# A four-layer graph megakernel: x loaded in chunks in turn, accumulating writes of one expert declared independent, and part of the edge counting placed under the first mixture

## The chip, the core and the metric

One Trainium2 chip, one core of it. The metric is the device time of one execution in microseconds (us). The kernel before takes 2444.24 us, the median of 8 runs (2439.33 to 2447.27).

TensorE (PE in the profile) multiplies matrices, VectorE (DVE) and ScalarE (ACT) work elementwise and empty the matmul accumulators (PSUM), GpSimd (POOL) does some elementwise work and issues the indirect transfers, and SyncE (SP) issues most plain transfers. Each engine runs its own queue of instructions in order, and semaphores tie the queues together.

## The reference

2708 nodes with 256 features each (`x`, f32) and a sparse 0/1 adjacency matrix pass through four layers. Each layer adds a graph block and then a feed-forward block, each on the layer norm of x:

```python
x = x + _L0_gnn_ref(_layernorm(x), adj, Wq, Wk)          # cosine attention over neighbours
x = x + _L0_ffn_ref(_layernorm(x)[None], ...)[0]         # pooled tokens through a state-space block
x = x + _L1_gnn_ref(_layernorm(x), adj, weight, bias)    # mean over neighbours, then a projection
x = x + _L1_ffn_ref(_layernorm(x)[None], ...)[0]         # first mixture: 8 experts, top 2
x = x + _L2_gnn_ref(_layernorm(x), adj, W, a)            # graph attention, 1 head
x = x + _L2_ffn_ref(_layernorm(x)[None], ..., edge_index)[0]  # second mixture, 4 experts
x = x + _L3_gnn_ref(_layernorm(x), adj, W, a)            # graph attention, 4 heads
x = x + _L3_ffn_ref(_layernorm(x)[None], ...)[0]         # third mixture: 8 experts with a capacity
```

Three pieces matter here. The first mixture is, for every expert `e` with hidden size 1024,

```python
h = gelu(xf @ W1[e] + b1[e])
out = out + w_dense[:, e:e+1] * (h @ W2[e] + b2[e])      # w_dense: softmax over the two best gates
```

The layer-2 attention projects the layer norm with a 256 x 256 matrix, scores each edge as leaky_relu(source + target), takes a softmax over the neighbours and aggregates.

The second mixture chooses its experts with a small attention over `edge_index`, a list of 1,048,576 (source, target) pairs drawn from 65,536 nodes. Only edges whose target is one of the 2708 nodes given here count; where the source is none of them either, it stands for a node whose features are zero. So for each target a count of such edges is needed (`cnt`), and the few edges with both ends inside are needed one by one.

## The kernel before

**x and the layer norm.** x stays in SBUF for the whole kernel as 22 tiles of 128 nodes (`self.x`, 128 x 22 x 256 f32; the last tile has 20 rows). Most passes go over `CHUNKS`, six chunks of up to 512 nodes (four tiles; the last has one full tile and the tail of 20). At the start (L52 to L64) the first four tiles come one by one, in turn from the queues of SyncE and ScalarE, and the rest as three transfers of four tiles, one of five and the tail, all of SyncE. The layer norm of a chunk is a statistic per tile on VectorE (`ln_st`, L1617, `ln_mv`, L1618), a square root on ScalarE and a reciprocal and a shift on VectorE (L1620 to L1622), and the scaled rows `fa` (L1629 on ScalarE, L1631 on VectorE). TensorE transposes `fa` (`ft_ps`, L1587; `f_ps` in layer 0), the copies `fT` empty it, and the projection follows (`wqk` in layer 0, L1706; `v_ps`, L3389, in layer 2).

**The first mixture, `fast_l1_ffn` (L3198).** Each of the eight experts has 768 slots: six tiles (`TPE`) of 128 tokens, handled as two halves of three tiles (`HT`). `Route` (from L2835) ranks the tokens, and writes for every slot the row to gather (`idg`) and the row to add to (`ids`). For a half, three indirect transfers on GpSimd gather the tokens (`xe`, L2954), TensorE transposes them (`xt_ps`, L3228; `turn`), `k.copy` empties the accumulator into `xT`, turn about on VectorE (L76) and ScalarE (L78), the up product runs (`h_ps`, L3242, 16 matmuls) with its gelu on ScalarE (`hT`, L3249), and the down product (`y_ps`, L3259, 24 matmuls). VectorE adds the bias and multiplies by the gate (`ys`, L3267 and L3268), and an indirect transfer on GpSimd adds each tile of `ys` to the rows of `acc` in DRAM (L3271), 48 such accumulating writes in all. `acc` holds x itself beforehand, so afterwards it is the new x. Empty slots point to spare rows behind the nodes' rows, one per partition (`p1n`, L2930, `number`, L2978). All these writes go to one tensor, so each waits for the landing of the one before. After the last, seven transfers of three tiles and the tail bring `acc` back into `self.x` (L3326 to L3333).

**The side work.** `Edges` finds and counts the edges of the second mixture. `search` (L2561) is a generator of eight steps: each loads a piece of `edge_index`, builds a key per edge inside the range, and takes the best 72 keys of each partition with nine rounds of maximum and replacement on VectorE (L2585, L2586), into `L`, 128 x 576. `count` (L2592) is a generator too. It splits the keys into the target's high and low part and the source (L2610 and on), takes the up to 32 keys per partition with both ends inside in four rounds, ranks them over partitions (`rank_oh`, L2686, `rank_oc`, L2693, `rank_ov` on GpSimd, L2701, 32 matmuls L2708), and then, for 18 groups of 32 key columns, builds two one-hot arrays on VectorE:

```python
                oh = hot.tile([128, HB, 128], BF16, name="oh")
                ol = hot.tile([128, HB, NT], BF16, name="ol")
                for out, val, n in ((oh, lob, 128), (ol, hib, NT)):
                    nc.vector.tensor_tensor(
                        out,
                        io[:, None, :n].to_broadcast([128, HB, n]),
                        val[:, s0 : s0 + HB, None].to_broadcast([128, HB, n]),
                        ALU.is_equal,
                    )
```

(L2745 to L2752), whose product, 32 matmuls of 22 columns (L2756), is added into `cnt_ps`. The one-hots have two buffers, so a pair waits for the matmuls of the pair two before. A copy gives `cnt`.

`fast_l1_ffn` is given `search` as its side work and takes one step after each expert (`next(side)`, L3323); the loop after it empties what is left. `count` is given to the layer-2 attention, `fast_gat` (L3336), which takes a step between its pieces.

**The layer-2 attention.** The preamble: weights and the small products `pr` and `w` (L3373, L3379), layer norm and projection of all chunks (`V`, `fs`), the maximum over nodes, exponentials, the scaling of `V` on GpSimd (L3416), and the spreading of the row values over partitions (`spread_ps`, L118; the copies `Rr`, L76 and L78). The body: for every chunk of targets and each of 21 source tiles an adjacency tile `aj` is loaded, VectorE makes `PT` (L3459), and TensorE adds `acc_ps` (L3528).

**What orders the work.** The engine queues are written by a tile framework whose recording layer lays out the instructions of several generators side by side by planned times; within one engine the order is fixed when the kernel is built. Dependences between instructions are found from the tiles that they touch.

Of the kernel before, what the change touches and what calls it, by code (L numbers as in the profile page):

```python
# [1 line left out]

# [5 lines left out]
F32 = mybir.dt.float32  # L8
# [4 lines left out]
ALU = mybir.AluOpType  # L13
# [30 lines left out]
class K:  # L44
# [3 lines left out]
    def __init__(self, ctx, tc, x_in):  # L48
# [6 lines left out]
        for t in range(4):  # L55
            (nc.scalar if t % 2 else nc.sync).dma_start(
                self.x[:, t, :], x_in[t * 128 : (t + 1) * 128]
            )
        for t0, n in ((4, 4), (8, 4), (12, 4), (16, 5)):
            nc.sync.dma_start(  # L60
                self.x[:, t0 : t0 + n, :],
                x_in[t0 * 128 : (t0 + n) * 128].rearrange("(t p) d -> p t d", p=128),
            )
        nc.sync.dma_start(self.x[:TAIL, NT - 1, :], x_in[(NT - 1) * 128 : N])  # L64
# [5 lines left out]
        nc.vector.memset(self.eps, 1e-5)  # L70

# [2464 lines left out]
class Edges:  # L2536
# [55 lines left out]
    def count(self):  # L2592
        nc, tc = self.k.nc, self.k.tc
        with tc.tile_pool(name="ep", bufs=1) as pp, tc.tile_pool(
            name="eh", bufs=2
        ) as hot, tc.tile_pool(name="ps_eh", bufs=1, space=PSUM) as ps:
# [53 lines left out]
            rp = ps.tile([128, 5 * OW], F32, name="rank_ps")  # L2650
# [93 lines left out]
            cp = ps.tile([128, NT], F32, name="cnt_ps")  # L2744
# [90 lines left out]
class Route:  # L2835
# [14 lines left out]
    def __init__(self, k, ctx, w, most):  # L2850
# [10 lines left out]
        self.acc = dram.tile([N + 1 + 128, D], F32, name="acc")  # L2861
# [22 lines left out]
        nc.gpsimd.dma_start(self.acc[N + 1 :, :], zero[:, :D])  # L2884
# [45 lines left out]
        self.p1n = pool.tile([128, 1], F32, name="p1n")  # L2930
        nc.vector.tensor_scalar(self.p1n, self.p1, float(N), None, ALU.add)
# [32 lines left out]
    def early(self):  # L2964

        v = self.k.nc.vector
        bad = self.k.bad[:, 6:7]
        v.tensor_scalar(bad, self.sofar[:, 0:1], -1.0, float(HT * 128), ALU.mult, ALU.add)
        f = self.one.tile([128, 2, HT], F32, name="early_f")
        idf, idp = f[:, 0, :], f[:, 1, :]  # L2970
        v.scalar_tensor_tensor(
            idf, self.slot_f[:, 1, :HT], 128.0, self.slot_f[:, 2, :HT], ALU.mult, ALU.add
        )
        self.number(idf, idp, self.idg0, self.ids0)
        self.xe0 = self.gather(self.idg0, self.most * 128 + 1)
        yield

    def number(self, idf, idp, idg, ids):  # L2978

        v = self.k.nc.vector  # L2980
        v.tensor_copy(idg, idf)
        v.tensor_scalar(idp, idf, 0.0, self.p1n, ALU.is_equal, ALU.mult)
# [215 lines left out]
def fast_l1_ffn(k, side, route, rest):  # L3198
# [8 lines left out]
    with ExitStack() as ctx:  # L3207
# [3 lines left out]
        ps1 = ctx.enter_context(tc.tile_pool(name="ps_f11", bufs=3, space=PSUM))  # L3211
        ps2 = ctx.enter_context(tc.tile_pool(name="ps_f12", bufs=2, space=PSUM))

        def psum():
            return pst.tile([128, 512], F32, name="xt_ps")

        class Half:
# [5 lines left out]
            def turn(self):  # L3223
                self.xT = dp.tile([128, 2, HC], F32, name="xT")
                for kk in range(2):
# [7 lines left out]
                    k.copy(self.xT[:, kk, :], tp[:, :HC])  # L3233
# [20 lines left out]
            def down(self):  # L3254
                _, _, w2t, b2t = route.weights[self.e]
                for i in range(HT):
# [14 lines left out]
                    nc.gpsimd.indirect_dma_start(  # L3271
# [7 lines left out]
                    )  # L3279
                    yield  # L3280
# [25 lines left out]
        side = side(route.start)  # L3306
        nxt = [one, half(0, 1)]
        run(first)
        for e in range(E):
# [13 lines left out]
            next(side)  # L3323
        for _ in side:
            pass
        for t0 in range(0, NT - 1, 3):  # L3326
            nc.sync.dma_start(
                k.x[:, t0 : t0 + 3, :],
                acc[1 + t0 * 128 : 1 + (t0 + 3) * 128].rearrange(
                    "(t p) d -> p t d", p=128  # L3330
                ),
            )
        nc.sync.dma_start(k.x[:TAIL, NT - 1, :], acc[1 + (NT - 1) * 128 : 1 + N])  # L3333
# [1090 lines left out]
def model(tc, I, out):  # L4424
# [4 lines left out]
    with tc.tile_pool(name="flags", bufs=1) as fp:  # L4429
# [4 lines left out]
        with ExitStack() as ctx:  # L4434
# [5 lines left out]
            with tc.tile_pool(name="lists", bufs=1) as lp:  # L4440
                edges = Edges(k, part(I, "L2_ffn_"), lp)
                order = (0, 1, 5, 2, 3, 4)
                with ExitStack() as c1:
# [18 lines left out]
                    fast_l1_ffn(k, edges.search, route, rest)  # L4462
                fast_gat(
                    k, adjT, I["L2_gnn_W"], I["L2_gnn_a"], 1, True, 2, edges.count()
# [76 lines left out]
```

## Time and profile before

| | us |
|---|---|
| median of 8 runs | 2444.24 (2439.33 to 2447.27) |
| the profiled run | 2442.74 |
| its span, first to last instruction | 2440.9 |
| mean granted TensorE clock | 0.952 |

The profiled run is one of the usual ones, 1.5 us under the median; 1.84 us of it lie outside the span. Of the span, this is what TensorE and VectorE are busy in each stage:

| stage | us from the start | length | TensorE busy | VectorE busy | clock |
|---|---|---|---|---|---|
| start and layer-0 projection | 0 to 60 | 60.0 | 43.99 | 40.98 | 1.00 |
| layer-0 attention | 60 to 340 | 280.0 | 280.00 | 117.10 | 1.00 |
| layer-0 feed-forward | 340 to 562 | 222.0 | 202.23 | 140.65 | 0.89 |
| layer-1 graph block, with most of the routing | 562 to 790 | 228.0 | 214.81 | 113.77 | 0.97 |
| end of the routing, start of expert 0 | 790 to 820 | 30.0 | 26.85 | 14.12 | 0.94 |
| rest of the first mixture, reload of x | 820 to 1184.7 | 364.7 | 334.84 | 259.50 | 0.97 |
| layer-2 attention, preamble | 1184.7 to 1238.3 | 53.6 | 36.72 | 50.90 | 0.75 |
| layer-2 attention, body | 1238.3 to 1465 | 226.7 | 221.47 | 210.66 | 0.99 |
| second mixture | 1465 to 1740 | 275.0 | 269.92 | 89.36 | 0.93 |
| layer-3 attention, start of the third mixture | 1740 to 2230 | 490.0 | 440.44 | 394.49 | 0.94 |
| rest of the third mixture | 2230 to 2440.9 | 210.9 | 194.27 | 105.66 | 0.97 |

A row of a timeline gives the start and the length in us, the engine, the source line, the operation, what it writes and reads, and how many instructions the row holds; in square brackets is the idle time of the engine before it and what ended that. A row of a window gives its bounds and length, the busy time of TensorE, of its weight load, of VectorE, ScalarE and GpSimd (instructions in brackets), the granted TensorE clock, the busy share of the DMA engines and GB/s. A group's row gives the smallest, median and largest duration in ns and the first and last start.

### The profile page before, as it was taken

The page shows a single profiled execution, that of the slowest core. Times are in us where ns is not written, and L with a number is a line of the kernel's source. Part 1 is how long each engine was busy: PE and PEld are TensorE (multiplying, and loading weights), DVE is VectorE, ACT ScalarE, POOL GpSimd, SP SyncE. Part 2 cuts the span into 40 slices and gives each one's busy share as a digit, 9 for nine tenths or more (in the row PEclk, how much of TensorE's full clock was granted, in tenths as well). Part 3 has the DMA queues.
Part 4 walks back from the last instruction along what each step waited for, and adds up shares of the span by engine and source line. Part 5 has one row for each costly group of instructions (what it writes and reads, how often), then busy time and mean ns, then how long its engine had stood idle before and what let it go on. Part 6 is the DMA issues. An engine that isn't in the chain of part 4 may idle for free. (4 is left out here: it accounts for less than half of the span.)

```text
span 2440.9 us, 31809 instructions
## 1 busy us (share of the span) xinstructions
PE 2265.6 (93%) x11620; PEld 1513.2 (62%) x11620; DVE 1537.2 (63%) x3419; ACT 659.3 (27%) x1329; POOL 419.5 (17%) x490
## 2 busy tenths in 40 slices
PE   7999999988999899999689999999889999968997
PEld 4677775677778566767578876666553333325665
DVE  6444338655446699961598994152579999863544
ACT  5433333214664222122310003232321111111121
POOL 2000003004000324332150001620030000002321
PEclk9999999879999899999889996999999999978998
DMA  4233322200664444341254423000024433315340
GB/s 129 65 99 96 100 61 77 74 1 11 217 210 131 144 111 118 86 95 24 65 166 128 145 54 58 21 1 1 10 67 116 117 113 112 95 43 170 118 133 14
DMA packets 158380, 219.34 MB, mean 90 GB/s; under 512 B 30879, under 2 KB 94083, under 8 KB 158212
## 3 DMA queue, kind: packets, MB, share of 16 engines
q1 hardware_dynamic: 125856, 179.58, 25.0%
q0 software_dynamic: 15248, 23.39, 4.6%
q10 hardware_dynamic: 17108, 14.22, 1.8%
q8 instruction: 96, 1.57, 0.3%
q14 instruction: 72, 0.59, 0.1%
HBM read 193.49 MB, written 24.17 MB: 89 GB/s over the span
## 5 line engine op out<-in xcount | busy, mean ns | idle before, releaser
L3459 DVE SCALAR_TENSOR_TENSOR PT<-Rr,Q,aj 128x512 f32<-128x512 f32 (+3 forms) x630 | 405.5, 702 | 25.5 <-PE acc_ps L3528 13.7
L3605 PE MATMUL acc_ps<-PT,V 128*64 128x512 f32 (+4 forms) x2016 | 328.5, 549 | 0.4 <-ACT Rr L78 0.4
L3605 PEld LDWEIGHTS acc_ps<-PT,V 128*64 128x64 f32 (+1 forms) x2016 | 95.2, 122 | 210.1 <-issue 154.6
L1819 PE MATMUL acc_ps<-fa,PT 128*128 128x257 f32 x882 | 213.9, 382 | 0.5 <-DVE PT L1793 0.5
L1819 PEld LDWEIGHTS acc_ps<-fa,PT 128*128 128x128 f32 x882 | 164.6, 190 | 63.8 <-issue 41.0
L3528 PE MATMUL acc_ps<-V,PT 128*128 128x257 f32 x882 | 198.6, 385 | 1.5 <-POOL V L3416 0.9
L3528 PEld LDWEIGHTS acc_ps<-V,PT 128*128 128x128 f32 x882 | 167.3, 192 | 28.5 <-DVE PT L3459 2.4
L3242 PE MATMUL h_ps<-xT,w1t 128*128 128x384 f32 x512 | 173.3, 497 | 5.1 <-DVE xT L76 4.9
L1793 DVE SCALAR_TENSOR_TENSOR PT<-aj,PT 128x512 f32<-128x512 int32 (+1 forms) x126 | 80.1, 643 | 147.8 <-ACT PT L1792 147.7
L3259 PE MATMUL y_ps<-w2t,hT 128*128 128x256 f32 x768 | 168.6, 379 | 0.0
L2478 PE MATMUL acc_ps<-V,at 128*128 128x257 bf16 x1323 | 157.9, 278 | 3.6 <-DVE at L2472 3.6
L3259 PEld LDWEIGHTS y_ps<-w2t,hT 128*128 128x128 f32 x768 | 145.4, 190 | 21.4
L2478 PEld LDWEIGHTS <-at 128*128 128x128 bf16 x1323 | 130.0, 100 | 26.5 <-issue 5.0
L3242 PEld LDWEIGHTS h_ps<-xT,w1t 128*128 128x128 f32 x512 | 97.8, 194 | 72.5 <-DVE xT L76 6.3
L1792 ACT ACTIVATE PT<-s_ps,rq 128x512 f32<-128x512 f32 (+1 forms) x126 | 79.4, 637 | 168.0 <-PE s_ps L1768 166.9
L3271 POOL DMA_INDIRECT acc<-ys,ids x48 | 77.8, 1620 | 237.8 <-DVE ys L3268 117.5
L1768 PE MATMUL s_ps<-KT,QT 128*128 128x512 f32 (+1 forms) x252 | 116.4, 546 | 0.9 <-POOL KT L1747 0.6
L3951 PE MATMUL y_ps<-w2t,hT 128*128 128x256 f32 (+1 forms) x528 | 117.2, 379 | 0.0
L3938 PE MATMUL h_ps<-fT,w1t 128*128 128x512 f32 (+1 forms) x288 | 116.4, 554 | 0.3 <-ACT hT L3945 0.2
L4374 PE MATMUL y_ps<-w2t,hT 128*128 128x256 f32 (+1 forms) x512 | 112.8, 379 | 0.0
L3951 PEld LDWEIGHTS y_ps<-w2t,hT 128*128 128x128 f32 (+1 forms) x528 | 97.7, 186 | 22.3 <-issue 8.2
L3249 ACT ACTIVATE hT<-h_ps,b1t 128x384 f32<-128x384 f32 x128 | 74.3, 581 | 108.9 <-PE h_ps L3242 108.7
(743 smaller groups left out, 3355.0 us busy)
## 6 DMA issues: line engine op xcount, KB each, us to landing
aj<-in_adjT SPq DMA_DIRECT2D x399, 256.0 KB
w1t<-in_L_ffn_W SPq DMA_DIRECT2D x8, 1024.0 KB
w2t<-in_L_ffn_W SPq DMA_DIRECT2D x8, 1024.0 KB
w1t<-in_L_ffn_w SPq DMA_DIRECT2D x8, 1024.0 KB
w2t<-in_L_ffn_w SPq DMA_DIRECT2D x8, 1024.0 KB
aj<-in_adjT SPq DMA_DIRECT2D x63, 74.0 KB
fd<-fa ACTq DMA_DIRECT2D x9, 512.0 KB
aj<-in_adjT SPq DMA_DIRECT2D x21, 202.0 KB
```

The costliest lines, as they stand in the source:

```text
L1768: nc.tensor.matmul(s[:, :cs], lhsT=QT[:, j * 128 : j * 128 + 128], rhs=KT[:, c0 : c0 + cs], start=True, stop=True,)
L1793: nc.vector.scalar_tensor_tensor(PT[p, :n], aj[p, :n], 0.0, PT[p, :n], ALU.is_gt, ALU.mult)
L1819: nc.tensor.matmul(ac, lhsT=PT[:, o : o + n], rhs=fa[:, j, :], start=j == 0, stop=False)
L2478: nc.tensor.matmul(ac[:, c:], lhsT=at[:, o : o + n], rhs=V[:, j, r], start=j == 0 and q == 0, stop=False, skip_group_check=True,)
L3242: nc.tensor.matmul(hp, lhsT=w1t[:, kk, m * 128 : (m + 1) * 128], rhs=self.xT[:, kk, :], start=(kk == 0), stop=(kk == 1),)
L3259: nc.tensor.matmul(y, lhsT=self.hT[:, m, i * 128 : (i + 1) * 128], rhs=w2t[:, m, :], start=(m == 0), stop=(m == M - 1),)
L3459: nc.vector.scalar_tensor_tensor(PT, R, Q, aj, ALU.max, ALU.mult)
L3528: nc.tensor.matmul(ac[:n], lhsT=PT[:, o : o + n], rhs=V[:, j, 0, :], start=(j == 0), stop=False,)
L3605: nc.tensor.matmul(w.pop("out"), **w)
L3938: nc.tensor.matmul(o[:, :cs], lhsT=w1t[:, kk, m * 128 : (m + 1) * 128], rhs=fT[:, kk, c0 : c0 + cs], start=(kk == 0), stop=(kk == 1),)
L3951: nc.tensor.matmul(y[:n], lhsT=hT[:, m, o : o + n], rhs=w2t[:, m, :], start=(m == 0), stop=(m == M - 1),)
L4374: nc.tensor.matmul(y[:n], lhsT=hT[:, m, o : o + n], rhs=w2t[:, m, :], start=(m == 0), stop=(m == M - 1),)
```

## The change

Five edits.

1. `load_x` loads x, at the start and again from `acc` after the first mixture, as six chunks (the last in two transfers), all on SyncE's queue. Each transfer waits for the landing of the one two before it.
2. `acc` gets a set of 128 spare rows for each of an expert's six tiles (five more transfers of zeros at the start), and an iota `spare` with the rows takes the place of `p1n`. With that no two writes of one expert touch the same row, and these are declared independent. The first write of an expert waits for all writes of the expert before, and the reload of x for all of the last expert's.
3. Both copies of `xT` go to ScalarE; `h_ps` has two accumulators in place of three, `y_ps` three in place of two.
4. `count` puts its tiles at the other end of the memory and uses one bank `edge_ps` for its accumulators. `search` and `count` are chained as one side work of the first mixture, of which 1, 1, 2, 1, 2, 1, 3 and 2 steps are taken after the eight experts: 13 steps, of which `search` has eight. The loop that empties the side work stands where it stood, ahead of the reload of x; the layer-2 attention is given the same (by then empty) generator.
5. `early` takes the maximum of a count and the half's size in place, instead of writing a difference into a check flag.

```diff
+    def load_x(self, src, also=None):
+        ld = []
+        for c0, cs in CHUNKS:
+            t0, n = c0 // 128, cs // 128
+            ld.append(
+                self.nc.sync.dma_start(
+                    self.x[:, t0 : t0 + n, :],
+                    src(slice(c0, c0 + n * 128)).rearrange("(t p) d -> p t d", p=128),
+                )
+            )
+            if cs % 128:
+                ld.append(
+                    self.nc.sync.dma_start(
+                        self.x[:TAIL, NT - 1, :], src(slice((NT - 1) * 128, N))
+                    )
+                )
+        for i, inst in enumerate(ld):
+            if also:
+                also(inst)
+            if i > 1:
+                self.tc.add_manual_dep(
+                    inst.ins,
+                    ld[i - 2].ins.name,
...
     def count(self):
-        with tc.tile_pool(name="ep", bufs=1) as pp, tc.tile_pool(
-            name="eh", bufs=2
-        ) as hot, tc.tile_pool(name="ps_eh", bufs=1, space=PSUM) as ps:
+        with tc.tile_pool(name="ep", bufs=1, side="right") as pp, tc.tile_pool(
+            name="eh", bufs=2, side="right"
+        ) as hot, tc.tile_pool(name="ps_eh", bufs=1, space=PSUM, side="right") as ps:
+            bank = ps.tile([128, 512], F32, name="edge_ps")
...
-        self.acc = dram.tile([N + 1 + 128, D], F32, name="acc")
+        self.acc = dram.tile([N + 1 + TPE * 128, D], F32, name="acc")
...
-        nc.gpsimd.dma_start(self.acc[N + 1 :, :], zero[:, :D])
+        for i in range(TPE):
+            nc.gpsimd.dma_start(self.acc[N + 1 + i * 128 : N + 129 + i * 128, :], zero[:, :D])
...
-        self.p1n = pool.tile([128, 1], F32, name="p1n")
-        nc.vector.tensor_scalar(self.p1n, self.p1, float(N), None, ALU.add)
+        self.spare = count("spare", [E, TPE], [[0, E], [128, TPE]], base=N + 1, mult=1)
...
-        v.tensor_scalar(idp, idf, 0.0, self.p1n, ALU.is_equal, ALU.mult)
+        spare = self.spare.rearrange("p e t -> p (e t)")[:, : idf.shape[1]]
+        v.scalar_tensor_tensor(idp, idf, 0.0, spare, ALU.is_equal, ALU.mult)
...
-        ps1 = ctx.enter_context(tc.tile_pool(name="ps_f11", bufs=3, space=PSUM))
-        ps2 = ctx.enter_context(tc.tile_pool(name="ps_f12", bufs=2, space=PSUM))
+        ps1 = ctx.enter_context(tc.tile_pool(name="ps_f11", bufs=2, space=PSUM))
+        ps2 = ctx.enter_context(tc.tile_pool(name="ps_f12", bufs=3, space=PSUM))
...
-                    k.copy(self.xT[:, kk, :], tp[:, :HC])
+                    nc.scalar.copy(self.xT[:, kk, :], tp[:, :HC])
...
+                    mine = adds.setdefault(self.e, [])
+                    for o in mine:
+                        tc.declare_no_dep(add.ins, o.ins, reason="rows of other tokens")
+                    if not mine:
+                        wait_for(add, adds.get(self.e - 1, []))
+                    mine.append(add)
...
-            next(side)
+            for _ in range((1, 1, 2, 1, 2, 1, 3, 2)[e]):
+                next(side)
         for _ in side:
             pass
-        for t0 in range(0, NT - 1, 3):
-            nc.sync.dma_start(
-                k.x[:, t0 : t0 + 3, :],
-                acc[1 + t0 * 128 : 1 + (t0 + 3) * 128].rearrange(
-                    "(t p) d -> p t d", p=128
-                ),
-            )
-        nc.sync.dma_start(k.x[:TAIL, NT - 1, :], acc[1 + (NT - 1) * 128 : 1 + N])
+        k.load_x(lambda r: acc[1 + r.start : 1 + r.stop], lambda ld: wait_for(ld, adds[E - 1]))
...
+                    def search(start):
+                        side.append(chain(edges.search(start), edges.count()))
+                        return side[0]
+
+                    fast_l1_ffn(k, search, route, rest)
                 fast_gat(
-                    k, adjT, I["L2_gnn_W"], I["L2_gnn_a"], 1, True, 2, edges.count()
+                    k, adjT, I["L2_gnn_W"], I["L2_gnn_a"], 1, True, 2, side[0]
                 )
```

## The prediction, made before the changed kernel ran

> **What bounds the kernel now.** I read the busy table and the slices first, then the span in windows by stage, then the timeline where TensorE stops, then single groups.
>
> ```profile
> span 2440.9 us, 31809 instructions
> PE 2265.6 (93%) x11620; PEld 1513.2 (62%) x11620; DVE 1537.2 (63%) x3419; ACT 659.3 (27%) x1329; POOL 419.5 (17%) x490
> ```
>
> TensorE works 93% of the span. Work taken off another engine is worth something only where TensorE stands still, 175 us in all. The windows (TensorE's busy time is the first number after the length) say where:
>
> ```profile
> 0.00:12.00 12.00, 0.05 (x1) 0.08 (x2) 5.35 (x27) 2.86 (x5) 8.95 (x39) 1.00 0.89 239
> 820.00:880.00 60.00, 49.14 (x184) 33.29 (x183) 51.40 (x81) 13.42 (x23) 28.44 (x21) 0.89 0.54 155
> 880.00:1130.00 250.00, 244.76 (x986) 181.15 (x985) 202.73 (x297) 54.49 (x97) 90.05 (x65) 1.00 0.41 96
> 1171.00:1184.00 13.00, 0.00 (x0) 0.00 (x0) 0.78 (x2) 0.00 (x0) 3.77 (x7) 0.63 0.34 59
> 1184.00:1238.00 54.00, 36.68 (x191) 29.51 (x191) 50.60 (x156) 23.14 (x54) 11.10 (x11) 0.75 0.30 95
> 1238.00:1300.00 62.00, 61.74 (x363) 53.52 (x364) 61.96 (x98) 4.87 (x10) 22.55 (x26) 0.96 0.54 162
> 1300.00:1450.00 150.00, 148.10 (x1129) 126.69 (x1127) 135.78 (x178) 5.83 (x14) 0.24 (x2) 1.00 0.38 113
> ```
>
> In order: the start; the first mixture (820 to 1171), nearly full on TensorE; 13 us in which TensorE does nothing; the preamble of the layer-2 attention; its body, full on TensorE, where VectorE is nearly full too but does not set the pace. The hole in the middle:
>
> ```profile
> 1171.48 0.35 DVE L3268 TENSOR_SCALAR ys<-ys,xe 128x256 f32<-128x256 f32 x1
> 1177.53 1.57 POOL L3271 DMA_INDIRECT acc<-ys,ids  x1 [2.90 <-DMA acc<-ys,ids]
> 1181.25 3.57 SPq L3327 DMA_DIRECT2D x<-acc  x7
> 1184.71 0.75 DVE L1617 BATCH_NORM_STATS2 ln_st<-x 128x6 f32<-128x256 f32 x2 [12.87 <-DMA x<-acc]
> ```
>
> The last product is done at 1171.83; two more accumulating writes follow, each issued only when the one before has landed; x is reloaded; the layer norm starts at 1184.71.
>
> **The change, term by term.** Sums are against the profiled run, span 2440.9 us, 2442.7 us in all, which is 1.5 us under the median of 2444.24.
>
> *The x loads at the start.* TensorE first runs at 11.95, waiting for `fa` of VectorE, which stood behind a layer-norm statistic that waited 1.31 us for x; its projection at 15.49 then waited 1.59 us for `wqk`, issued after all of x. In the changed order no statistic of a third chunk stands ahead of `fa`, and `wqk` is issued after the second chunk: 1.3 + 1.6, about **-2.8**. Against it, x's first piece is 512 KB, not 128 KB, 1.6 us more at the 239 GB/s of the first row, and a load waits for the landing of the one two before it. Behind these waits on SyncE's queue stand `wqk` and the first adjacency loads (before at 6.99), which nothing needs until the scores at 30 us. Bounds -5 and +3.
>
> *Accumulating writes.* Their waits cost GpSimd, not TensorE: a write with its wait takes 1.57 + 2.9 = 4.5 us, but six writes of an expert (27 us) fit in the 41 us that an expert takes. What they hold up are the gathers of tokens behind them on GpSimd's queue:
>
> ```profile
> 833.56 1.09 PE L3228 MATMUL xt_ps<-ident,xe 128*128 128x128 f32 x4 [6.48 <-DMA xe<-fd,idg]
> ```
>
> The write at 825.90 waited 3.02 us before the gathers that this transpose waits for; I take the 2.2 us of it that no other wait covers: **-2.2** (0 to -6.5). Putting both xT copies on ScalarE (0.48 us each, in place of 0.55 on a VectorE full of search work) ends the 4.9 us that the up products waited for VectorE's xT; half of it, **-2.5** (+1 to -4.9), since the two copies now follow each other. The first write of an expert now waits for all six of the one before, issued some 20 us earlier (the two up halves are 10.6 us each): no new wait, and its gathers stand ahead of it. The five extra zero writes go out while GpSimd waits for nothing; they are hidden by the L0 stage, and cost at most 5 x 0.52 us.
>
> *The counting pulled under the mixture.* Of 18 pairs of one-hots (`oh` and `ol`), 13 steps of the side work hold the search and the first five steps of the count. In the built order VectorE splits the lists and makes two pairs (some 26 us in all) during experts 5 and 6, does the rank part after the last `ys` of expert 6, and two more pairs during the up of expert 7. These cost nothing there: VectorE was idle 75.5 of the 86 us from 1085 to 1171 (without that cover they'd cost their 26 + 11 us). But **14 pairs stand on VectorE's queue after the last `ys` and ahead of the layer norm**, because the loop that empties the side work still stands ahead of the reload of x. A pair:
>
> ```profile
> L2749 DVE TENSOR_TENSOR oh<-io,lob x18: 4410/4415/4805, 1212.4 to 1443.9; 128x4096 bf16<-128x4096 bf16 x18
> L2749 DVE TENSOR_TENSOR ol<-io,hib x18: 876/882/1300, 1227.6 to 1448.3; 128x704 bf16<-128x704 bf16 x18
> L2701 POOL TENSOR_TENSOR rank_ov<-rank_oc,part x4: 1062/1290/1618, 1269.1 to 1272.7; 128x512 bf16<-128x512 bf16 x4
> ```
>
> 4.415 + 0.882 = 5.297 us, 14 of them 74.2 us, and the small operations of `pr`, `w` and the copy of `cnt` behind them (2 x 0.74 x 2, 0.2) 3.2 us: 77.4. They need TensorE only for counting products (32 per pair, 0.9 us), so nothing slows them. Before, 12.9 us lay between the last `ys` and the layer norm; the faster writes (about 5 us less) and the reload (3.5 us) now lie wholly under the pairs. So **+64.5**. Upper end: `oh` took 4.805 and `ol` 1.300 while GpSimd was scaling V; at that price all pairs would add 11.3 more. Lower end: 62, if the copy of `cnt` is free.
>
> The Trainium skill, page "VectorE: DVE Perf Modes", section "The perf-mode tier table", gives a bf16 `tensor_tensor` in SBUF the double rate, 2048 elements in 1224 ns. By it (an estimate) a pair would take 2.87 us, the block 40 us, and the whole sum come to about -2. The row above has 4096 elements in 4.415 us, 0.93 per ns, so the double rate is not reached here (the same page's "What auto-detection actually checks" wants steps of one, and both operands are broadcast). I go by the row.
>
> *Inside the last expert's up.* 13 of 16 up products are done at about 1137.0 (1128.4 + 13 x 0.66); then 32 rank products stand on TensorE's queue and wait for four `rank_ov` on GpSimd, which wait for VectorE: last `ys` of expert 6 at 1128.6, small operations 1.3, `rank_oh` 4.4, `rank_oc` and `part` 0.9, then 4 x 1.3: 1140.4. Stall **+3.4** (0 to +6). Moved in with it: rank products 1.1 us, 64 counting products 1.8: **+2.9**. Behind them wait the last up products, so the last down.
>
> *The preamble of the attention.* From layer norm to the first aggregation it was 1238.26 - 1184.71 = 53.55 us. Leaving are the counting operations from 1206.75 on, above all the `oh` at 1212.38 and at 1229.46 (4.8 us), behind which the copies of the spread row waited until 1234.2. v_ps ended at 1222.5, 37.8 after the layer norm. Of the 15.8 us from there to the first aggregation I leave 5 for the maximum, the spread products and the first PT: 43 in place of 53.55, **-10.5** (-6 to -14).
>
> *The body.* Counting products leave TensorE: 16.9 us over all windows, 1.5 of them before 1238, plus rank products 1.1 and about 3 us of waiting for `ol` and at `PT`: **-19.5** (-15 to -25). VectorE loses some 95 us there and TensorE stays the bound.
>
> *The second mixture's start.* A few small operations of `par`, `dhi`, `dlo` move ahead: **-1.5** (0 to -3).
>
> Sum: -2.8 - 2.2 - 2.5 + 64.5 + 3.4 + 2.9 - 10.5 - 19.5 - 1.5 = **+31.8**. Span 2472.7; on the median 2444.2 + 31.8 = **2476**.
>
> **The rivals.** *The pairs get under the mixture after all (faster).* VectorE is idle 75.5 of the 86 us from 1085 to 1171, and that is room for 14 pairs. If they ran there, the 64.5 would go, 5 us of write tail would leave the hole, and 15.1 us of counting products would enter the mixture: -2.8 + 1.6 + 15.1 - 5 - 10.5 - 19.5 - 1.5 = -22.6, so 2422. The side that it falls on turns at a block of 74.2 - 31.8 = 42.4 us, eight pairs: seven of the 14 would have to slip ahead of the last `ys`. Against it: an engine's queue runs in the order built. Chance 4%.
>
> *The writes did hold the mixture up.* TensorE is idle 10.9 us of 820 to 880 and 5.2 of 880 to 1130; freed gathers return all 16.1 in place of 4.7: 11.4 less, 2465. Against it: much of that idleness stands before VectorE's search work. Chance 10%.
>
> *The block is dearer.* Pairs at the slow price, 11.3 more, from GpSimd's last writes or any contention: 2487. Against it: only two of 18 were so slow, and GpSimd is idle through most of the block. Chance 16%.
>
> **How the numbers follow.** The forecast has 70%. The terms' bounds taken together come to some 12 us either way (2464 to 2488); the range reaches to the two neighbours beside it, 2457 to 2493. A measurement tells 0.2%, about 5 us, from no change. Faster 0.04 is the first rival; same 0.02; slower 0.94.
>
> **What would show it.** In the profile after: 14 `oh` in a row between the last `ys` and the first layer-norm statistic, about 77 us in which TensorE runs only short bursts; no wait before `x<-acc` for the last write; a body of the attention some 20 us shorter; TensorE waiting for `rank_ov` in the last up. I am wrong if the layer norm starts less than 55 us after the last `ys`, or if the body of the attention is no shorter, which would put VectorE or the adjacency loads at its bound, and the time near 2495.

## The result, and the profile after

The changed kernel takes 2456.36 us, the median of 13 runs (2445.81 to 2459.6), where the kernel before takes 2443.3 (38 runs): 1.0047 times, with a 95% interval of 1.0037 to 1.0056. Measured once more on another occasion it was 1.0032 times (1.0021 to 1.0044). It is slower, as forecast, by some 8 to 13 us in place of 32; 2456.4 lies just under the forecast range (2457 to 2493).

The page of the profiled run (span, then busy time, share of the span and instructions of each engine):

```profile
span 2458.3 us, 31810 instructions
PE 2256.3 (92%) x11620; PEld 1508.3 (61%) x11620; DVE 1534.7 (62%) x3402; ACT 666.3 (27%) x1347; POOL 432.9 (18%) x496
```

TensorE is busy 9 us less and the span is 17.4 us longer: the time went into TensorE standing still. The windows of the changed kernel by stage show where:

```profile
0.00:12.00 12.00, 1.94 (x8) 1.57 (x8) 6.94 (x32) 4.50 (x8) 10.67 (x34) 1.00 0.87 258
809.80:870.00 60.20, 54.43 (x213) 37.73 (x213) 50.33 (x95) 15.78 (x29) 30.03 (x23) 0.94 0.53 155
1119.00:1161.50 42.50, 40.77 (x250) 30.76 (x249) 19.50 (x31) 8.64 (x16) 11.90 (x9) 1.00 0.12 13
1161.50:1237.20 75.70, 15.88 (x513) 15.79 (x511) 75.45 (x40) 0.00 (x0) 7.55 (x11) 0.52 0.19 48
1237.20:1279.30 42.10, 33.33 (x157) 26.11 (x157) 28.07 (x123) 22.66 (x53) 5.38 (x9) 0.84 0.10 29
1279.30:1480.00 200.70, 200.45 (x962) 168.00 (x962) 118.86 (x244) 13.20 (x28) 17.65 (x22) 1.00 0.50 141
```

The fourth row is the new hole: for 75.7 us VectorE (the third busy time) is busy 75.45 and TensorE 15.88. The last two rows are the attention's preamble, 42.1 us, and its body, 200.7 us at 99.9% of TensorE. The timeline of the changed kernel over the hole, both ends of it:

```profile
1162.18 0.35 DVE L3308 TENSOR_SCALAR ys<-ys,xe 128x256 f32<-128x256 f32 x1
1162.51 4.43 DVE L2773 TENSOR_TENSOR oh<-io,lob 128x4096 bf16<-128x4096 bf16 x1
1162.81 5.54 POOL L3311 DMA_INDIRECT acc<-ys,ids  x1 [1.91 <-DVE ys L3308]
1166.85 0.88 DVE L2773 TENSOR_TENSOR ol<-io,hib 128x704 bf16<-128x704 bf16 x1
1167.65 4.42 DVE L2773 TENSOR_TENSOR oh<-io,lob 128x4096 bf16<-128x4096 bf16 x1
1171.31 0.93 SPq L71 DMA_DIRECT2D x<-acc  x2
...
1229.30 4.42 DVE L2773 TENSOR_TENSOR oh<-io,lob 128x4096 bf16<-128x4096 bf16 x1
1233.64 0.88 DVE L2773 TENSOR_TENSOR ol<-io,hib 128x704 bf16<-128x704 bf16 x1
1234.44 0.75 DVE L3415 TENSOR_TENSOR pr<-w,ar 128x256 f32<-128x256 f32 x2
1237.18 0.74 DVE L1640 BATCH_NORM_STATS2 ln_st<-x 128x6 f32<-128x256 f32 x2
```

The reload of x starts at 1171.31, and the layer norm could follow it; it comes at 1237.18, behind 14 pairs on VectorE's queue (the block, as it is called below).

Lengths of stages, read off the first start of the same group in each profile (us; "ys to layer norm" is from the start of the last `ys`):

| run | end of layer-0 attention to end of layer-1 aggregation | mixture: first `y_ps` to last `ys` | last `ys` to layer norm | layer norm to first aggregation | body | body to second mixture | span |
|---|---|---|---|---|---|---|---|
| before, three profiles | 429.6, 425.1, 431.5 | 356.8, 357.2, 357.3 | 13.2, 13.4, 13.1 | 53.6, 57.0, 53.5 | 221.9, 221.9, 222.3 | 39.6, 39.6, 39.5 | 2440.9, 2441.4, 2446.0 |
| changed, two profiles | 427.5, 423.2 | 352.4, 352.4 | 75.0, 75.0 | 42.1, 42.3 | 200.6, 200.5 | 35.8, 34.6 | 2458.3, 2452.5 |
| counting alone | 423.9 | 370.8 | 75.0 | 42.1 | 200.6 | 35.6 | 2476.7 |
| all, counting back, tiles new | 419.2 | 347.7 | 8.7 | 78.2 | 212.2 | 39.6 | 2429.9 |
| all, counting as before | 429.6 | 348.1 | 8.6 | 57.1 | 221.6 | 39.6 | 2429.0 |
| no emptying loop | 426.4 | 352.5 | 12.8 | 81.8 | 204.3 | 34.2 | 2434.8 |
| pairs early | 430.2 | 392.4 | 10.0 | 45.5 | 202.2 | 34.6 | 2439.5 |
| pairs in the body | 424.9 | 352.7 | 8.3 | 46.8 | 216.6 | 37.4 | 2410.2 |
| writes alone | 425.6 | 357.2 | 8.1 | 55.4 | 222.1 | 39.5 | 2436.7 |
| xT and accumulators alone | 427.5 | 347.1 | 13.0 | 53.9 | 222.5 | 39.5 | 2432.5 |
| xT copies alone | 423.3 | 348.4 | 13.4 | 53.8 | 222.5 | 39.5 | 2431.5 |
| accumulators alone | 431.2 | 365.9 | 13.2 | 55.8 | 222.2 | 39.5 | 2452.1 |
| x loads alone | 427.9 | 357.6 | 14.1 | 57.3 | 221.6 | 39.5 | 2440.2 |

The first column is work that the edits hardly touch, and it wanders by 12 us over these executions; this limits what one profile's span can say (the section on more profiles shows what it goes with). The other columns repeat within half a microsecond where a kernel was profiled more than once, except the one with the layer norm (3.5 us over three profiles of before) and the last stage (1.2).

### The profile page after: what moved, and what is told of

Its sections match the earlier page's. It is cut to its first block, busy times and chain, and to the rows that moved or that the text cites. A ratio compares the mean times of both kernels' runs of the same rounds, so it can differ in the third digit from the quotient of the medians.

```text
span 2458.3 us, 31810 instructions
## 1 busy us (share of the span) xinstructions
PE 2256.3 (92%) x11620; PEld 1508.3 (61%) x11620; DVE 1534.7 (62%) x3402; ACT 666.3 (27%) x1347; POOL 432.9 (18%) x496
## 5 line engine op out<-in xcount | busy, mean ns | idle before, releaser
L3311 POOL DMA_INDIRECT acc<-ys,ids x48 | 87.5, 1823 | 206.9 <-DVE ys L3308 174.0
```

## The experiments

Ratios are to the kernel before, measured on the same chip in turn, with 95% intervals.

**Counting alone.** The kernel before, with edit 4 and nothing else:

```diff
-            next(side)
+            for _ in range((1, 1, 2, 1, 2, 1, 3, 2)[e]):
+                next(side)
...
-                    fast_l1_ffn(k, edges.search, route, rest)
+                    fast_l1_ffn(k, search, route, rest)
```

> The kernel before with only the counting moved: search and count chained as the mixture's side work in the same steps, the loop that empties them left ahead of the reload of x; x loads, accumulating writes, xT copies and accumulators as before. Theory (the 14 pairs of one-hots on VectorE ahead of the layer norm are the loss, and the counting brings all that the layer-2 attention gains): +62 between last ys and layer norm (less if the write tail was longer), -11 preamble, -21 body, -4 second mixture's start, +5 rank and counting products in the mixture: about +30, so 2473. Rival (the faster mixture came from the counting's new places, not from writes, xT or accumulators): mixture some 6 us shorter, about +18, so 2461.

Measured: 2478.79 us, 1.0146 (1.0128 to 1.0164). Block, preamble and body are those of the changed kernel to 0.1 us. The mixture is 14 us longer than before, where the theory had 5 and the rival a shorter one, so the time is 6 us above the theory's. TensorE's waits of more than 0.8 us after 900 us, from the timeline of this run (the bracket is TensorE's idle time and what ended it):

```profile
950.87 12.28 PE L3244 MATMUL h_ps<-xT,w1t 128*128 128x384 f32 x32 [3.25 <-DVE xT L77]
1042.89 6.48 PE L3244 MATMUL h_ps<-xT,w1t 128*128 128x384 f32 x14 [2.81 <-DVE xT L77]
1143.72 1.09 PE L2710 MATMUL edge_ps<-rank_ov,rank_oh 128*128 128x64 bf16 x32 [3.03 <-POOL rank_ov L2703]
```

The loss belongs to the counting, and more than all of it: the other edits gave some 24 us back (1.0146 against 1.0047). The up products wait for `xT` on VectorE; in the changed kernel, with these copies on ScalarE (edit 3), no such wait is left.

**Counting taken back.** The changed kernel with the two side works as before:

```diff
-            for _ in range((1, 1, 2, 1, 2, 1, 3, 2)[e]):
-                next(side)
+            next(side)
...
-                        side.append(chain(edges.search(start), edges.count()))
-                        return side[0]
+                        side.append(edges.count())
+                        return edges.search(start)
```

> The changed kernel with the counting given back to the layer-2 attention (one step of the search after each expert, count among the attention's pieces). Theory: start -2.7, mixture -6.6 and another -4.9 since rank and counting products are not in it, last ys to layer norm 7.6 us in place of 12.9, so -5.3: about -19 in all, 2424; the preamble is 53 us and the body 222 again. Rival (the mixture's gain hangs on the counting's move): start and write tail alone, -8, so 2435.

Measured: 2438.75 us, 0.9975 (0.9961 to 0.9989). A miss: 15 us above the theory's number, near the rival's, but not for the rival's reason, since the mixture got shorter still (347.7). The preamble had grown from 53.6 to 78.2. A window from the first `v_ps` to the first aggregation, and the same window with VectorE's one-hots alone (busy time, number):

```profile
1168.60:1235.40 66.80, 43.54 (x398) 35.14 (x398) 63.17 (x100) 18.43 (x46) 14.15 (x8) 0.73 0.11 35
1168.60:1235.40 66.80, 46.82 (x17) 0.73 0.11 35
```

17 one-hot operations, 46.8 us of VectorE, had been put among the projection. The next run asks why.

**All but the counting.** The same, with the counting's tiles and accumulators where they were before:

```diff
-        with tc.tile_pool(name="ep", bufs=1, side="right") as pp, tc.tile_pool(
-            name="eh", bufs=2, side="right"
-        ) as hot, tc.tile_pool(name="ps_eh", bufs=1, space=PSUM, side="right") as ps:
-            bank = ps.tile([128, 512], F32, name="edge_ps")
+        with tc.tile_pool(name="ep", bufs=1) as pp, tc.tile_pool(
+            name="eh", bufs=2
+        ) as hot, tc.tile_pool(name="ps_eh", bufs=1, space=PSUM) as ps:
...
```

> The changed kernel with all of the counting as before (steps, its tiles' side of the memory and its accumulators): x loads, accumulating writes, xT copies alone. The run that kept the tiles on the other side had 66.8 us from the first v_ps to the first aggregation, with ten pairs among the layer norm and projection, where the kernel before has 42.8. Theory (the tiles' place lets the planner draw the pairs forward into the preamble, and each then costs there what it takes on VectorE): first v_ps to first aggregation 43, body 222, so 14 less than that run: 2425. Rival (the earlier x or the shorter write tail draws the pairs forward): 66 us again, 2438.

Measured: 2426.72 us, 0.9926 (0.9908 to 0.9943), and 46.0 us from the first `v_ps` to the first aggregation. The window of the one-hots there:

```profile
1180.00:1226.00 46.00, 10.11 (x3) 0.76 0.16 50
```

Three operations in place of 17. So the place of the tiles (their side of the memory, the accumulator's bank, or both; these weren't taken apart) decides how early the recording layer may put a pair, and early was worse by 12 us.

**No emptying loop.** The changed kernel without two lines:

```diff
-        for _ in side:
-            pass
```

> The changed kernel without the loop that empties the side work ahead of the reload, so that what is left of the count goes to the layer-2 attention. In the built order 2 pairs stand between the last ys and the layer norm, 3 among the layer norm, 7 ahead of the first PT, 2 in the body. Theory (a pair costs 5.1 us wherever it stands on VectorE ahead of something TensorE waits for): block about 13 us, preamble 53 to 80 us, body some 18 shorter than before: 2425 to 2440. Rival (pairs cost only because TensorE had nothing to do beside them; among the layer norm they hide): preamble 45, about 2405.

Measured: 2438.86 us, 0.9979 (0.9967 to 0.9991), as the theory had it. The block is gone (12.8), and layer norm to first aggregation takes 81.8 us where 80 were expected: the pairs only moved from the front of the preamble into it. The window of that preamble:

```profile
1173.70:1255.50 81.80, 46.12 (x477) 38.60 (x476) 77.98 (x140) 23.23 (x55) 14.08 (x8) 0.71 0.19 59
```

VectorE is full again, 77.98 of 81.8. Taking away the two lines wins 13 to 17 us (0.9979 against the changed kernel's 1.0032 and 1.0047), no more.

**Pairs early.** The steps after the eight experts:

```diff
-            for _ in range((1, 1, 2, 1, 2, 1, 3, 2)[e]):
+            for _ in range((1, 1, 2, 1, 2, 12, 9, 0)[e]):
```

> The changed kernel with the steps after the eight experts 1, 1, 2, 1, 2, 12, 9, 0 in place of 1, 1, 2, 1, 2, 1, 3, 2: in the built order all 18 pairs stand ahead of the last ys. Theory (the block is the loss; VectorE has some 80 us free in experts 6 and 7 for 103 us of work): last ys to layer norm about 8 us, preamble 42, body 200, mixture longer by 14 us of counting products and 10 to 30 us of waits for ys: 2415 to 2437. Rival (one-hots beside GpSimd's gathers and writes cost much more, as the last accumulating write took 5.5 us beside an oh): mixture 50 us longer, 2450 or more.

Measured: 2439.58 us, 0.9971 (0.9961 to 0.9982). That is 2.6 us above the theory's range, with a mixture at the long end of what the theory had. All pairs stood under the mixture, which became 40 us longer than the changed kernel's (392.4): TensorE is busy 18 us longer in it (361.2 for 343.2, 15 of them in the counting's matmuls) and idle 22 us longer (31.2 for 9.2). The last 92 us of it:

```profile
1113.00:1205.00 92.00, 74.28 (x724) 58.97 (x722) 85.46 (x66) 11.02 (x20) 29.78 (x15) 0.89 0.12 14
```

VectorE 85.46 of 92, TensorE idle 17.7, most of it in four waits of 4.11 to 4.13 us for `ol`: the idle time of VectorE under two experts was too little for all 18 pairs. This is the first rival of the prediction, built as a kernel. It paid 40 us for the 65 that it saved, and came out faster than before by 0.29%, not by the 22 us worked out there, which had the pairs find room at no price.

**Pairs in the body.** The loop away, as are the four steps that the attention took after each chunk, and each of the 14 pairs tied behind a PT of the body, one for seven:

```diff
-                    nc.vector.tensor_tensor(
+                    hot_op = nc.vector.tensor_tensor(
...
+                    gate = getattr(self.k, "gate", None)
+                    if gate is not None:
+                        tc.add_manual_dep(
+                            hot_op.ins,
+                            gate.ins.name,
...
-        for _ in side:
-            pass
...
-            nc.vector.scalar_tensor_tensor(PT, R, Q, aj, ALU.max, ALU.mult)
+            k.gate = nc.vector.scalar_tensor_tensor(PT, R, Q, aj, ALU.max, ALU.mult)
...
                     PT = weights(c0, cs, j, 0, adjacency(c0, cs, j))
+                    if (i * (NT - 1) + j) % 7 == 4:
+                        next(side, None)
...
-                for _ in range(4):
-                    next(side, None)
```

> The changed kernel without the loop that empties the side work, and each of the 14 left pairs tied behind a PT of the attention's body, one for seven PTs. Theory (a pair is free only where TensorE has other work queued): last ys to layer norm 8.7, preamble 42 as in the changed kernel, body 200.6 + 14 x 0.9 + a few waits = 216: 2405. Rival (VectorE is too full in the body, where PT and pairs together need some 175 us of 216 and a pair of 5.1 us holds up PT): body 230, 2420.

Measured: **2411.9 us, 0.9871 (0.9849 to 0.9893)**: faster than both kernels, and 7 us above the theory's number. Windows of the hole, the preamble and the body:

```profile
1159.60:1167.60 8.00, 0.75 (x30) 0.65 (x26) 0.01 (x1) 0.00 (x0) 2.17 (x6) 0.69 0.48 119
1167.60:1214.40 46.80, 35.24 (x157) 28.00 (x158) 28.12 (x119) 23.13 (x54) 6.04 (x10) 0.80 0.27 83
1214.40:1431.00 216.60, 212.59 (x1409) 179.38 (x1410) 188.89 (x280) 12.22 (x28) 21.86 (x26) 1.00 0.45 130
```

The body is 216.6 as worked out: 14 pairs cost 16 us there, 1.14 each, of which 0.9 are TensorE's counting products, and VectorE, at 188.89 of 216.6, doesn't take the bound. The preamble, 46.8, is 4.7 longer than the changed kernel's; 4.1 of that lie ahead of the first `v_ps`, where x's chunks now land during the layer norm. The theory had 42 for it.

**The other edits, one at a time.** Writes alone, xT copies with accumulators, xT copies alone, accumulators alone, x loads alone, each put into the kernel before:

```diff
-                    k.copy(self.xT[:, kk, :], tp[:, :HC])
+                    nc.scalar.copy(self.xT[:, kk, :], tp[:, :HC])
```

```diff
-        ps1 = ctx.enter_context(tc.tile_pool(name="ps_f11", bufs=3, space=PSUM))
-        ps2 = ctx.enter_context(tc.tile_pool(name="ps_f12", bufs=2, space=PSUM))
+        ps1 = ctx.enter_context(tc.tile_pool(name="ps_f11", bufs=2, space=PSUM))
+        ps2 = ctx.enter_context(tc.tile_pool(name="ps_f12", bufs=3, space=PSUM))
```

> The kernel before with only the accumulating writes changed (spare rows per tile, writes of one expert independent, the reload of x waiting for the last expert's six). Theory (the writes held up the gathers of the second expert, and the last two stood ahead of the reload): mixture 3 to 5 us shorter, last ys to layer norm 8.7 in place of 13.2: -8 to -10, so 2435. Rival (the mixture's gain is that of the xT copies): the 4.5 us of the tail alone, 2440.

Measured: 2437.04, 0.9978 (0.9967 to 0.9988). The rival: the mixture is as long as before (357.2), and 5.1 us of the tail is all. In the timeline the wait that I had laid to the writes stands there unchanged (before: 6.48), and so does the first for `xT`:

```profile
832.08 1.09 PE L3243 MATMUL xt_ps<-ident,xe 128*128 128x128 f32 x4 [6.67 <-DMA xe<-fd,idg]
861.95 7.44 PE L3257 MATMUL h_ps<-xT,w1t 128*128 128x384 f32 x17 [2.12 <-DVE xT L76]
```

> The kernel before with only the xT copies on ScalarE and the accumulators of the up and down products at 2 and 3. Theory: the up products' waits for VectorE's xT (2.1 + 0.8 us in the rows over 0.8) end, mixture 3 to 5 us shorter: 2440. Rival (nothing but what the writes bring): no change, 2444.

Measured: 2434.25, 0.9968 (0.9954 to 0.9981), twice the gain expected. The mixture is 9.7 us shorter, and the waits for the gathers (6.48 and 0.86 before) are shorter with it, though the writes are as before; from its first `y_ps` on, TensorE's only waits over 0.8 us are these two:

```profile
830.77 0.74 PE L3228 MATMUL xt_ps<-ident,xe 128*128 128x128 f32 x2 [3.54 <-DMA xe<-fd,idg]
832.69 1.12 PE L3228 MATMUL xt_ps<-ident,xe 128*128 128x128 f32 x4 [1.18 <-DMA xe<-fd,idg]
```

> The kernel before with only the xT copies on ScalarE, accumulators 3 and 2 as before. Theory (VectorE, full of search work, held up the up products through xT): mixture 350 of 356.8, 2437. Rival (the third accumulator of the down product did it): mixture 355, 2442.

Measured: 2438.93, 0.9978 (0.9969 to 0.9987); mixture 348.4: near the theory's 2437 and 350. The gathers' waits are as short as with both edits (3.53 and 1.18), so they came with the copies alone. The first `y_ps` starts at another place in each of these kernels; from the end of the layer-1 aggregation to the last `ys` it is 369.9, before 376.0 and with both edits 366.4. Of the 3.5 us between the last two, 1.5 are a wait of the down product for `ys` on VectorE, which neither of the other two kernels has.

> The kernel before with only the accumulators of the up product at 2 and of the down product at 3. Theory (xT copies did it): mixture within 2 of 356.8, 2441 to 2444. Rival (a third accumulator takes in VectorE's lateness at ys, which TensorE otherwise waits for): mixture 350, 2436.

Measured: 2451.01, 1.0023 (1.0012 to 1.0034): slower, which neither theory had. From the end of the layer-1 aggregation to the last `ys` it is 378.6, before 376.0; the up products still wait 5.2 us for VectorE's `xT`, before 4.9. What grew are the waits for the gathers, 10.9 us for 7.3, with this one above all:

```profile
833.80 1.58 POOL L3271 DMA_INDIRECT acc<-ys,ids  x1 [5.69 <-DVE a L2575]
839.07 0.66 PE L3228 MATMUL xt_ps<-ident,xe 128*128 128x128 f32 x2 [8.33 <-DMA xe<-fd,idg]
```

The second expert's gathers start at 835.68, behind an accumulating write for which GpSimd waited 5.69 us: its `ys`, at 833.54, stands on VectorE's queue behind two operations of the search, the first of which waited 2.45 us for its load. In these profiles the third accumulator of the down product pays only with the copies off VectorE; the times alone don't say so, since the intervals with it (0.9954 to 0.9981) and without (0.9969 to 0.9987) overlap.

> The kernel before with only the x loads changed, at the start and after the first mixture (there still behind all writes). Theory (first transpose and wqk earlier): start -2.7, the reload after the mixture about the same as before: 2439. Rival (the chunks' waits for landings cost at the reload what they bring at the start): layer norm to first v_ps 2 to 3 longer, 2442.

Measured: 2442.39, 0.9994 (0.9983 to 1.0005): no change that can be told. The start is 4.1 us earlier (first aggregation of layer 0 at 30.7, before at 34.8); the layer norm to the first aggregation of layer 2 takes 57.3, just above before's 53.5 to 57.0. The number is the rival's; whether the reload gave the start's gain back is not settled by it.

**More profiles.** The changed kernel once more, and the kernel before twice, since the stages of the first two profiles add up to more than the medians differ:

> The changed kernel once more, to have a second profile of it and its times beside the others' on one chip. Theory: last ys to layer norm 75 and preamble 42 within 0.5 in this profile too, mixture 350 to 353; the time 11 to 14 above before. Rival (the layer-0 feed-forward's and the mixture's lengths wander by some 5 us from one execution to the next, and part of the stage readings is that): the mixture's length differs from 352.4 by more than 3.

> The kernel before once more, for a second profile. The two profiles of the changed kernel differ by 4.3 us between the end of the layer-0 attention and the first expert (427.5 and 423.2), and by 0.1 at most in the mixture, the block, the preamble and the body together. Theory (that stretch wanders from execution to execution in both kernels, and the first profile of before, 429.6, was near its long end): 424 to 428 here, and from the first expert to the end within 1.5 of the first profile's 1645.4. Rival (the stages that the change touches wander as much): the mixture, preamble or body differ by more than 2.

> As the run before it, a third profile: theory 424 to 428 for the stretch, rival the same.

Measured: 2452.16, 1.0032 (1.0021 to 1.0044), 8 us above before and not 11 to 14; the stages that the change touches came out the same to 0.2 us, but for the 1.2 us at the second mixture's start. For the kernel before, the untouched stretch was 425.1 and 431.5 (forecast 424 to 428 for both: right once). Mixture and body repeated to 0.5 us, but the layer norm to the first aggregation took 57.0 and 53.5, so there the rival held: one of the touched stages wanders too, and why stays open.

The untouched stretch wanders with the granted TensorE clock. Windows of it in the third profile of before, its longest, and in the run with the counting taken back, its shortest:

```profile
367.10:798.60 431.50, 398.65 (x2580) 307.70 (x2579) 242.99 (x650) 169.73 (x416) 61.39 (x87) 0.92 0.33 102
361.30:780.50 419.20, 389.48 (x2580) 301.02 (x2579) 242.01 (x650) 168.82 (x416) 61.46 (x87) 0.95 0.34 105
```

With the same 2580 matmul instructions TensorE is busy 9.2 us longer at 0.92 than at 0.95. In all sixteen profiles the stretch's length times its clock (taken to three places) is 396.8 to 399.5 us, while the length alone goes from 419.2 to 431.5. What sets the clock there isn't shown.

## Why the prediction was right in direction and too high

The mechanism held: the 14 pairs on VectorE's queue ahead of the layer norm, the shorter preamble, the shorter body, the wait for `rank_ov`. The last write, at 1162.81, waits for its `ys` and no longer for the landing of the write before. Of the eight terms one was met, one was forecast too fast (the gathers), and six too slow, among them all the large ones. Measured values are from the first pair of profiles and, for the mixture, from the runs that separate it:

| term of the sum | forecast | measured | from |
|---|---|---|---|
| x loads at the start | -2.8 | -2.8 | first layer-0 aggregation 34.8 to 32.0 |
| gathers behind the writes | -2.2 | 0 | writes alone: 357.2 for 356.8 |
| xT copies and accumulators | -2.5 | -9.7 | xT and accumulators alone: 347.1 |
| wait for `rank_ov`, rank and counting products | +6.3 | +4.3 | 352.4 for 348.1 with the counting as before |
| block | +64.5 | +61.8 | 75.0 for 13.2 |
| preamble | -10.5 | -11.5 | 42.1 for 53.6 |
| body | -19.5 | -21.3 | 200.6 for 221.9 |
| second mixture's start | -1.5 | -3.8 | 35.8 for 39.6 |
| sum | +31.8 | +17.0 | the spans differ by 17.4 |

That the x loads met their term is luck of the first pair: over the eight profiles with the old loads and the eight with the new, the first layer-0 aggregation comes at 36.0 and 31.4 us on average, 4.6 earlier, which would bring the sum to +15.2.

Of the 14.8 us by which the sum was too high, 5.0 are the gathers and the xT copies together, 2.7 the block, 2.3 the second mixture's start, 2.0 the rank and counting products, 1.8 the body and 1.0 the preamble. The last two and the second mixture's start were sized too small; what made them larger was not taken apart.

**The step that failed most** is "half of it, **-2.5**" for the xT copies, with the -2.2 for the gathers that I laid to the writes. From the end of the layer-1 aggregation to the last `ys` TensorE was idle 19.8 us of 376.0 in the kernel before, and 11.3 of 366.4 with xT and accumulators alone. Adding the brackets of over 0.1 us in the two timelines says where: waits for `xT` 7.8 and 3.3 us (of the first, 4.9 for VectorE's copies, all gone), waits for the gathers 7.3 and 4.7, the rest 3.9 and 2.7. So the whole 4.9 came back and not half, at 0.4 for the copies following each other; and the gathers' 2.6 came with the same edit (the row numbers `idg` that they need were written 27.7 us after the end of the layer-1 aggregation, before 29.9), not through the writes, under which that wait stood unchanged. Why the row numbers come earlier is not shown. Another 1.1 us is TensorE's own busy time. The longest of the waits for `xT`, in the kernel before:

```profile
863.13 11.31 PE L3242 MATMUL h_ps<-xT,w1t 128*128 128x384 f32 x29 [2.12 <-DVE xT L76]
```

The second rival, a mixture that gets back more of TensorE's idle time, was right in the amount's direction and wrong in its cause.

**The block** was over-sized by 2.7, and 2.2 of it are the pairs: one takes 5.14 us from start to start (71.93 us from 1162.51 to 1234.44 for 14), not the 5.297 of two durations added, because each operation starts 0.08 us or so before the one ahead of it is over. The third rival (a dearer pair) fell: in the changed kernel's profile all 18 are alike:

```profile
L2773 DVE TENSOR_TENSOR oh<-io,lob x18: 4401/4415/4426, 1074.4 to 1229.3; 128x4096 bf16<-128x4096 bf16 x18
L2773 DVE TENSOR_TENSOR ol<-io,hib x18: 869/881/884, 1080.7 to 1233.6; 128x704 bf16<-128x704 bf16 x18
```

The same rows answer the Trainium skill's "VectorE: DVE Perf Modes", section "The perf-mode tier table": its double rate for bf16 operands isn't reached by these broadcast ones (4096 elements in 4.415 us, 0.93 per ns), and the sum by it, near -2, would have been the wrong sign.

**The wait for `rank_ov`** was 1.73 us in place of 3.4; 1.1 us of that is the four operations, which took 4.14 us together and not 5.2:

```profile
1120.76 4.14 POOL L2725 TENSOR_TENSOR rank_ov<-rank_oc,part 128x512 bf16<-128x512 bf16 x4 [4.64 <-DVE rank_oc L2717]
1124.95 1.09 PE L2732 MATMUL edge_ps<-rank_ov,rank_oh 128*128 128x64 bf16 x32 [1.73 <-POOL rank_ov L2725]
```

**The rest** lies between the profile and the median. The profiled run of the changed kernel, 2460.14 us, is the slowest of 15, its median 2456.4; the second profile spans 2452.5. The first pair of profiles differs by 17.4 us. That the table's sum lies so near is in part chance: between these two the untouched first column went down by 2.1, and the mixture's rows of the table give 351.4 where 352.4 was measured. The means of three and two spans differ by 12.6 (2455.4 - 2442.8), with the untouched column 3.4 shorter in the changed kernel's. So the stages ask for 15 to 17 us and the medians show 8 to 13. The stretch that goes with the clock moves by more than that from one execution to the next, but that it makes the difference between two medians isn't shown; 2 to 9 us stay open.

The range was made from bounds of the terms as if they missed independently, and they missed together.

## What to carry to other kernels

A side work's price is set by where the recorder puts it: the same pairs cost 5.1 us each ahead of a layer norm, about 3.5 among a projection (ten of them, 81.8 for 46.8 us), and 1.1 behind a queue of matmuls; when work is pulled forward, look for the loop that still empties the rest, and tie what is left to the stage that can hide it. When an engine is saturated by side work, its small copies on the main path are the first thing to move off it, and their price is found by trying them alone, not by one row's idle time. Several edits in one change can hide each other's loss: here two that gain 0.3% and 0.2% and a third that loses 1.5% made +0.3% to +0.5%.

## What was not expected of the hardware

An indirect transfer's issue on GpSimd takes 1.62 us for a write and 1.08 for a gather (medians of the changed kernel's mixture). The three that began there while a large one-hot operation, `oh` of 4.4 us, ran on VectorE ended only after it, and took 4.8 to 5.8 us. GpSimd's rows and VectorE's, of the changed kernel's timeline:

```profile
1074.46 5.77 POOL L3311 DMA_INDIRECT acc<-ys,ids  x1 [0.30 <-issue]
1080.54 1.56 POOL L3311 DMA_INDIRECT acc<-ys,ids  x1 [0.30 <-issue]
1082.40 1.08 POOL L2979 DMA_INDIRECT xe<-fd,idg  x1 [0.30 <-PE xt_ps L3268]
1083.79 4.79 POOL L2979 DMA_INDIRECT xe<-fd,idg  x1 [0.31 <-issue]
```

```profile
1074.40 4.40 DVE L2773 TENSOR_TENSOR oh<-io,lob 128x4096 bf16<-128x4096 bf16 x1
1083.24 4.41 DVE L2773 TENSOR_TENSOR oh<-io,lob 128x4096 bf16<-128x4096 bf16 x1
```

The write at 1074.46 and the gather at 1083.79 are two of the three; the write at 1080.54, with no `oh` beside it, takes 1.56, and the gather at 1082.40, which began 0.84 us before an `oh`, takes 1.08. The last write of the changed kernel is the third, 5.54 us at 1162.81. What holds them isn't shown. In the kernel before no such issue in the mixture took over 2.2 us. So one-hots under a mixture also delay its writes and gathers; with the four pairs that the changed kernel has there it cost nothing that can be told, since the 4.3 us that its mixture is longer than with the counting as before are about what the rank and counting products and their wait take (1.09 + 1.76 + 1.73).
